# Performer on one Trainium2 core: ScalarE's square of a projection moved ahead of VectorE's rotation products, with a new order of all steps

## The chip, the cores and the metric

The kernel runs on one core of one Trainium2 chip. The metric is the time of one execution in device microseconds (us). Shorter is better. The engines are TensorE (PE, with its weight load PEld), VectorE (DVE), ScalarE (ACT), GpSimd (POOL) and SyncE (SP), which issues most transfers.

## What is computed

The program is a network of four layers on an input of 8 x 128 x 16 x 16, all in float32: an adder convolution, a Mamba layer of three scan branches, a layer of softmax attention with a mixture of experts, and a performer of eight layers with a spectral filter after it. The change lies in the attention of the performer. Per layer `i`, cut to what matters:

```python
q = (t @ Wq[i] + bq[i]);  k = (t @ Wk[i] + bk[i]);  v = (t @ Wv[i] + bv[i])
rot = stack((-t2[..., 1], t2[..., 0]))          # pairs of features exchanged
q = q * cos + rot(q) * sin                       # rotary, the same for k
dd   = (data * dn) @ proj.T                      # data: q or k, per head
diag = sum(data * data, -1) * 0.5 * dn * dn
out  = ratio * (exp(dd - diag - max(dd)) + eps)  # random features
ctx  = kp.T @ v;  o = (qp @ ctx) / (qp @ sum(kp))
t = t + o @ Wo[i] + bo[i];  t = t + gelu(layer_norm(t) @ W1) @ W2 + b2
```

A rotation does not alter the sum of squares of a pair, so the kernel takes `diag` from the square of the projection before it is rotated. That is why the square and the two rotation products read the same projection.

## The kernel before

The 2048 tokens are four blocks of 512 (two images each). A block is a Python generator, `_block`, which yields after each small step. It runs the third layer (`_layer2`), then eight performer layers (`_attention`, then the feed-forward part), then the end of the performer. Block 0 also prepares the weights of the next layer (`_weights_of`).

The order of the work is written out by hand: `AHEAD` runs thirty steps each of blocks 0 and 1 beside the Mamba layer, and then `ORDER`, a string of 1092 digits, says which block makes its next step. In it PE, DVE, ACT and POOL keep the order in which the steps were recorded (`manual_schedule`). So each engine works through one fixed queue, and an instruction that waits holds those behind it. A step of one block is never ahead of an earlier step of the same block; what the digits choose is how the four blocks interleave.

In `_attention`, `rotated(name)` is called for the key and, in the next step, for the query. It multiplies the normed state `u` by the weights into a bank of PSUM (`pa`), makes the two products with sine and cosine on VectorE (`ro`, L1565, and `rk` or `rq`, L1566), squares the projection on ScalarE (`sqk`, `sqq`; recorded at L1181 by the helper `act`), exchanges the pairs of `ro` (L1571) and adds (L1573). The step after the query's is the one that reads both squares:

```python
    pl = bank(S, [P, P], "pl3")
    for n, sq in enumerate((sqk, sqq)):
        for c in range(4):
            S.mm(pl[...], S.c("sel")[...], sq[:, c * P : (c + 1) * P], ...)
```

Each block has its own pools. `many` has three buffers for the tag "t", and `lsq3` (the squares of the state), `ro3`, `sqk`, `sqq`, and later `rd` take turns in them. `bank` takes one of the block's two PSUM banks. A helper `tables` loads another table on ScalarE when an activation needs a function that the present one lacks (exponential and logarithm in one, Gelu and tanh in the other); the page gives these loads the line L1173. All matmuls are recorded at L289.

Of the kernel before, what the change touches and what calls it, by code (L numbers as in the profile page):

```python
# [10 lines left out]
F32 = mybir.dt.float32  # L11
AF = mybir.ActivationFunctionType
# [4 lines left out]
P = 128  # L17
# [3 lines left out]
BLK = 512  # L21
# [270 lines left out]
def bc(ap, axis, n):  # L292

    a = ap.unsqueeze(axis)
    shape = list(a.shape)
    shape[axis] = n
    return a.to_broadcast(shape)
# [641 lines left out]
class _Fuse:  # L939
# [23 lines left out]
    def bank(self, shape, name):  # L963
        return self.psum.tile(shape, F32, tag="f", name=name)
# [133 lines left out]
def performer_layer(E, W):  # L1098
# [49 lines left out]

AHEAD = [t for i in range(30) for t in range(2) if i < (30, 30)[t]]
ORDER = [int(t) for t in (  # L1150
    "3203203322300231310203001302130303103023103020031203123012211001102001200310213200113301011301330203"
    "3203320312231233032123231223123233332332312312331231313232133213323032232202312320312021312221022110"
    "1322110231230212001020112032131303113023310032000201323001303202301201022120212033201320332203321300"
    "3200221022031022310233120020130012321031032100323003130130310320031033103201130323303021101120113301"
    "1332101220212002130212132301203222032200300220120112203210031203231010320011210130201130302101310230"
    "2101311301231013211022313223123132132133220133213003132103130221322013022013120231211312003121230032"
    "1103201230233110211331020001013002113001201032022320323021303323203220332130302002210220310223102312"
    "3002013001232103103210032300313030131030230103310320113012112002330133202212132320332113103131203031"
    "0231022023220122302230023210020313201320123312030323102132300300323313003311033112302012201330123122"
    "1031013121201220113210102002230220130221302113200203100321301230213031203102300201323100103320233320"  # L1160
    "20331031320132212032321023112222322132132213211201231123121021021132121312121013220130100213"
)]


# [4 lines left out]
def tables(S, name):  # L1169

    if S.table["now"] != name:
        S.table["now"] = name
        S.tc.keep_in_program_order(S.nc.scalar.preload_act_table_set(name))  # L1173


def act(S, out, src, func, **kw):
    if func in (AF.Exp, AF.Ln):
        tables(S, LN_EXP)
    elif func in (AF.Gelu, AF.Tanh):
        tables(S, GELU)  # L1180
    S.nc.scalar.activation(out, src, func, **kw)  # L1181
# [268 lines left out]
def _squares(S, h):  # L1450
    sq = S.many.tile([P, BLK], F32, tag="t", name="lsq3")
    act(S, sq, h, AF.Square)
    return sq
# [93 lines left out]
def _attention(S, i, H, sq, u, sums):  # L1547
# [6 lines left out]
    nc, one, two, many = S.nc, S.one, S.two, S.many  # L1554
# [4 lines left out]
    def rotated(name):  # L1559
        pa = bank(S, [P, 2, L], "pa3")  # L1560
        S.mm(pa.rearrange("p b l -> p (b l)"), w[name], u)
        bias = S.v(f"b{name}{i}")
        r = one.tile([P, 2, L], F32, tag="r" + name, name="r" + name)
        o = many.tile([P, 2, L], F32, tag="t", name="ro3")
        nc.vector.scalar_tensor_tensor(o, pa, bias, bc(S.c("sin"), 1, 2), ALU.add, ALU.mult)  # L1565
        nc.vector.scalar_tensor_tensor(r, pa, bias, bc(S.c("cos"), 1, 2), ALU.add, ALU.mult)  # L1566

        sq = many.tile([P, BLK], F32, tag="t", name="sq" + name)
        act(S, sq, pa.rearrange("p b l -> p (b l)"), AF.Square, bias=bias)
        o = o.rearrange("p b l -> p (b l)")  # L1570
        nc.vector.stream_shuffle(o, o, EXCHANGE)  # L1571
        r = r.rearrange("p b l -> p (b l)")
        nc.vector.tensor_add(r, r, o)  # L1573
        return r, sq

    k, sqk = rotated("k")
    yield
    q, sqq = rotated("q")

    ub = one.tile([P, 2, PAIR], F32, tag="ub", name="ub3")  # L1580
# [154 lines left out]
    sq = _squares(S, H)  # L1735
# [184 lines left out]
```

## Time and profile before

| what | value |
|---|---|
| median of 3 runs | 3007.63 us (3004.27 to 3009.06) |
| profiled execution | 3000.94 us, its span 2999.2 us |
| granted TensorE clock | 0.989 |
| busy in the span | PE 2854.1, DVE 2419.8, ACT 2273.2, POOL 699.6 us |
| loads of a ScalarE table | 134 in the profile, mean 1283 ns |
| a rotation product (L1565, L1566) | 744 and 742 ns, 64 of each |
| exchange and sum (L1571, L1573) | 723 and 692 ns, 64 of each |
| a square (`sqk`, `sqq`) | 684 and 682 ns, 32 of each |

The durations come from the one profiled execution. The span runs from the first to the last instruction of the profile. Time stands in order of the stages: the adder layer to about 1000 us, Mamba to about 1700, then the third layer and the performer to about 2760, then the spectral layer. In the tables of waits, "A <- B" says that A's engine stood idle and that B ended that. A busy PE is modelled: its matmuls are pipelined.

### The profile page before, as it was taken

How to read it: one execution, taken by the hardware profiler on the slowest of the kernel's cores; microseconds unless marked ns; L12 is line 12 of the kernel's file. 1: busy time of each engine (PE TensorE's matmuls, PEld its weight loads, DVE VectorE, ACT ScalarE, POOL GpSimd, SP SyncE). 2: the span in 40 equal slices, each digit the busy share in tenths (PEclk: the TensorE clock that was granted, in tenths of full speed). 3: DMA queues.
4: the chain of work that ended last, by engine and by line, in shares of the span. 5: the costliest groups of instructions: out<-in, count | busy, mean ns of one | idle time of the engine just before them, and what ended most of it. 6: DMA issues, size and time to landing. Idle time of an engine off the chain costs nothing.

```text
span 2999.2 us, 41845 instructions
## 1 busy us (share of the span) xinstructions
PE 2854.1 (95%) x16404; PEld 1275.4 (43%) x16404; DVE 2419.8 (81%) x3398; ACT 2273.2 (76%) x2744; POOL 699.6 (23%) x415
## 2 busy tenths in 40 slices
PE   9999999999999788998898998999999999999999
PEld 4222222222223333443343454455655555654444
DVE  8999999999997999999899658887777787784110
ACT  8999999999997777778777435578778778777332
POOL 0000000000000889998999400000000000000100
PEclk9999999999999999999999999999999999999999
DMA  2000000000000444344344200000000000001100
GB/s 68 1 1 5 1 1 5 1 2 5 1 1 16 169 149 148 135 149 141 133 157 137 84 29 1 14 1 14 14 14 1 14 14 1 14 1 53 43 29 14
DMA packets 39482, 133.46 MB, mean 44 GB/s; under 512 B 7522, under 2 KB 10732, under 8 KB 37748
## 3 DMA queue, kind: packets, MB, share of 16 engines
q1 hardware_dynamic: 38164, 129.46, 12.5%
q8 instruction: 129, 2.11, 0.3%
q10 hardware_dynamic: 1120, 1.32, 0.1%
q14 instruction: 69, 0.57, 0.1%
HBM read 127.88 MB, written 1.84 MB: 43 GB/s over the span
## 4 chain that ended last, share of the span: by engine, by line
PE 70%; DVE 16%; ACT 7%; POOL 3%; issue 3%; DMA 1%; DVEq 0%; ACTq 0%; POOLq 0%
PE o L289 30%; PE p L289 10%; DVE st L909 5%; PE acc L289 5%; PE g L289 4%; PE conv L289 3%; PE pc L289 2%; PE var L289 2%; PE pf L289 2%; POOL dbu L814 2%; PE pq L289 2%; PE pconv L289 1%; PE pn L289 1%; PE pa L289 1%; ACT da L827 1%
## 5 line engine op out<-in xcount | busy, mean ns | idle before, releaser
L289 PE MATMUL o<-d,sel 128*32 128x512 f32 x8512 | 921.5, 593 | 2.1 <-DVE d L446 1.2
L452 ACT ACTIVATE d<-sh,w 128x2048 f32<-128x2048 f32 x472 | 899.3, 1993 | 25.4 <-PE o L289 25.1
L450 DVE TENSOR_SCALAR d<-sh,w 128x2048 f32<-128x2048 f32 x592 | 718.4, 1281 | 11.0 <-PE o L289 10.9
L814 POOL TENSOR_TENSOR dbu<-du,bs 128x1024 f32<-128x1024 f32 x191 | 446.4, 2363 | 975.6 <-DVE du L786 970.1
L289 PEld LDWEIGHTS o<-d,sel 128*32 128x32 f32 x8512 | 278.6, 110 | 644.2 <-issue 523.0
L909 DVE TENSOR_TENSOR_SCAN st<-da,dbu 128x512 f32<-128x512 f32 x384 | 446.2, 1206 | 17.9 <-POOL dbu L814 13.8
L289 PE MATMUL acc<-st,cst 128*128 128x512 f32 x768 | 375.4, 621 | 52.8 <-DVE st L920 52.6
L827 ACT ACTIVATE da<-delta,neg_a 128x510 f32<-128x510 f32 x384 | 256.8, 684 | 79.1 <-DVE st L909 73.8
L289 PEld LDWEIGHTS acc<-st,cst 128*128 128x128 f32 x768 | 144.6, 196 | 252.7 <-issue 144.0
L920 DVE TENSOR_TENSOR st<-st,pcs 128x1024 f32<-128x1024 f32 x168 | 205.2, 1221 | 18.9 <-ACT pcs L819 1.6
L446 DVE SCALAR_TENSOR_TENSOR d<-sh,w,d 128x2048 f32<-128x2048 f32 x88 | 206.8, 2350 | 1.9
L1855 ACT COPY ug<-p 128x512 f32<-128x512 f32 x128 | 74.9, 585 | 136.7 <-PE p L289 136.7
L1173 ACT ACT_TABLE_LOAD x134 | 171.9, 1283 | 2.4
L1396 POOL TENSOR_TENSOR lw<-lw,turn 128x640 f32<-128x640 f32 x8 | 10.0, 1255 | 685.6 <-DVE turn L1395 592.6
L819 ACT COPY pcs<-cs 128x512 f32<-128x512 f32 x168 | 97.7, 582 | 54.2 <-DVE st L920 48.4
L289 PE MATMUL conv<-pad,f 128*128 128x512 f32 x288 | 135.0, 596 | 0.9 <-ACT pad L1071 0.5
L289 PE MATMUL p<-un,lw 128*128 128x512 f32 x256 | 123.7, 605 | 3.8 <-DVE un L1467 2.1
L289 PE MATMUL p<-g,lw 128*128 128x512 f32 x256 | 116.4, 597 | 3.9 <-ACT g L1181 3.9
L289 PE MATMUL p<-T,H 128*128 128x512 f32 x256 | 113.0, 600 | 0.8 <-DVE H L1784 0.8
L289 PE MATMUL g<-ug,me 128*128 128x512 f32 (+1 forms) x320 | 112.0, 509 | 0.0
L1181 ACT ACTIVATE ex<-ex 128x352 f32<-128x352 f32 x128 | 62.4, 494 | 51.6 <-DVE ex L1664 50.4
L289 PE MATMUL pf<-lw,rk 128*128 128x352 f32 x256 | 97.2, 476 | 0.5 <-DVE ek L1614 0.3
(366 smaller groups left out, 3898.6 us busy)
## 6 DMA issues: line engine op xcount, KB each, us to landing
bs<-rows SPq DMA_DIRECT2D x96, 512.0 KB, 3.8
cs<-rows SPq DMA_DIRECT2D x96, 512.0 KB, 4.6
m<-in_Mphi SPq DMA_DIRECT2D x8, 1024.0 KB, 4.9
lw<-in_layers SPq DMA_DIRECT2D x8, 948.0 KB, 4.7
f<-in_fuse SPq DMA_DIRECT2D x2, 1152.0 KB, 9.9
T<-in_T SPq DMA_DIRECT2D x1, 2064.0 KB, 7.4
diag<-in_diag SPq DMA_DIRECT2D x1, 1920.0 KB, 7.5
total<-sums SPq DMA_DIRECT2D x16, 64.0 KB, 2.0
```

The source lines that it names most:

```text
L289: self.nc.tensor.matmul(out, lhsT=lhsT, rhs=rhs, start=start, stop=stop)
L446: nc.vector.scalar_tensor_tensor(d, tap(k), wk, d, ALU.max, ALU.add)
L450: nc.vector.tensor_scalar(d, tap(k), wk, None, ALU.max)
L452: nc.scalar.activation(d, tap(k), AF.Abs, scale=-1.0, bias=wk)
L814: nc.gpsimd.tensor_tensor(dbs[r], got[r // NST]["du"], bc(row("bs", r), 1, 2), ALU.mult)
L819: nc.scalar.copy(pcs[r], row("cs", r))
L827: nc.scalar.activation(das[g % 3][:, :, 1:], d[:, :, 1:], AF.Exp, scale=a)
L909: nc.vector.tensor_tensor_scan(st[:, h, :], da, dbs[r][:, h, :], 0.0, ALU.mult, ALU.add)
L920: nc.vector.tensor_tensor(st, st, bc(pcs[r][:, :], 1, 2), ALU.mult)
L1173: S.tc.keep_in_program_order(S.nc.scalar.preload_act_table_set(name))
L1181: S.nc.scalar.activation(out, src, func, **kw)
L1855: nc.scalar.copy(dst, p4)
```

## The change

In `rotated`, the allocation of the square's buffer and the square itself now stand ahead of the two products and of their buffers. The string `ORDER` is a new one, of the same length and with the same number of each digit. Nothing else differs; the products are L1568 and L1569 in the changed file.

```diff
 ORDER = [int(t) for t in (
-    "3203203322300231310203001302130303103023103020031203123012211001102001200310213200113301011301330203"
+    "3203320320230231310231310032103210113132113200323020110302100123032102110031000113001320113322011303"
...
 )]
...
         pa = bank(S, [P, 2, L], "pa3")
         S.mm(pa.rearrange("p b l -> p (b l)"), w[name], u)
         bias = S.v(f"b{name}{i}")
+
+        sq = many.tile([P, BLK], F32, tag="t", name="sq" + name)
+        act(S, sq, pa.rearrange("p b l -> p (b l)"), AF.Square, bias=bias)
         r = one.tile([P, 2, L], F32, tag="r" + name, name="r" + name)
         o = many.tile([P, 2, L], F32, tag="t", name="ro3")
         nc.vector.scalar_tensor_tensor(o, pa, bias, bc(S.c("sin"), 1, 2), ALU.add, ALU.mult)
         nc.vector.scalar_tensor_tensor(r, pa, bias, bc(S.c("cos"), 1, 2), ALU.add, ALU.mult)
-
-        sq = many.tile([P, BLK], F32, tag="t", name="sq" + name)
-        act(S, sq, pa.rearrange("p b l -> p (b l)"), AF.Square, bias=bias)
         o = o.rearrange("p b l -> p (b l)")
         nc.vector.stream_shuffle(o, o, EXCHANGE)
```

More of the change, by code (lines that the diff above doesn't have):

```diff
@@ L1150 @@
 ORDER = [int(t) for t in (
-    "3203203322300231310203001302130303103023103020031203123012211001102001200310213200113301011301330203"
[L1152 to L1161, printed above, removed]
+    "3203320320230231310231310032103210113132113200323020110302100123032102110031000113001320113322011303"
+    "1133123001322302132321322332123323133230330213230123323233220230223322332230320320020133222032103210"
+    "2320011203002302021010212033023230300332003102103030113301210123013113320331103312301322132200231232"
+    "0302210032020030220302213032203123021332313031000200230311002103102110131201201230120133131131133121"
+    "3013210312232020320312300030231002032012032122020312001322012312023003320033211003210113021130323332"
+    "3320130221330232203232210323201132201320010011021210101310312010203010322010213003312231301331323101"
+    "2321012132001133101201033202101302110320112101201133203322113103132120201321201302200120200102201022"
+    "3101220132102311213011030020201010330230130233013320320310233121133113320313103321301322132200231232"
+    "0310220023020030202302231032203120231332310330100200320311002103120110311201123021132033210112112231"
+    "2133220321310312010202301120301020203100220120103122001103121123121310321230323123003113023312331131"
+    "13321321103032311020332212320213213020132212232203221022022032312203212112321032030232031322"
 )]
```

## The prediction

> **What bounds the kernel now.** I read the engine table first, then the busy time by stage, then waits and the chain of waits inside the stage the diff touches.
>
> ```profile
> span 2999.2 us, 41845 instructions
> PE 2854.1 (95%) x16404; PEld 1275.4 (43%) x16404; DVE 2419.8 (81%) x3398; ACT 2273.2 (76%) x2744; POOL 699.6 (23%) x415
> PE   9999999999999788998898998999999999999999
> ```
>
> TensorE works 95% of the span. The edit and the digit string act on the performer, roughly 1750 to 2750 us; layers 0 and 1 and the spectral layer keep their instructions.
>
> ```profile
> 1750.00:2000.00 250.00, 231.68 (x1047) 122.23 (x1046) 182.04 (x551) 124.16 (x222) 8.30 (x21) 0.99 0.04 13
> 2000.00:2250.00 250.00, 241.80 (x1459) 144.87 (x1459) 194.12 (x484) 193.51 (x309) 5.92 (x12) 0.99 0.04 13
> 2250.00:2500.00 250.00, 243.33 (x1465) 142.86 (x1464) 188.20 (x470) 197.80 (x313) 8.88 (x18) 0.99 0.02 9
> 2500.00:2750.00 250.00, 243.80 (x1402) 140.51 (x1401) 175.87 (x433) 196.88 (x308) 2.96 (x6) 1.00 0.02 8
> ```
>
> The columns are window, length, then busy time of PE, PEld, DVE, ACT, POOL. Over these 1000 us PE is busy 960.6, DVE 740.2 and ACT 712.4, so DVE idles 260 and ACT 288. PE sets the time, and only its waits can be won. A busy PE hides short gaps, so I also took the start of every matmul row from the timeline and subtracted the usual spacing of its form (429 ns for 128x512 pieces): between 1750 and 2760 us, 97 gaps exceed 0.3 us and hold **63.6 us**. Most shorter ones recur with the form (256 in `pn`, 49 us) and no order removes them.
>
> Now who waits at the squares (answer of the waits view: engine, tile, line <- releaser: total us, times, longest):
>
> ```profile
> ACT sqk L1181 <- DVE rk L1566: 26.1, 22, 5.5
> ACT sqq L1181 <- DVE rq L1566: 14.8, 16, 1.5
> PEld pl L289 <- ACT sqq L1181: 8.9, 9, 2.0
> PE pl L289 <- ACT sqq L1181: 6.6, 6, 1.7
> ```
>
> ScalarE stands 40.9 us in 38 cases because VectorE has not finished its second product from the same projection `pa`, and then TensorE waits for ScalarE. The chain of waits shows both ways on:
>
> ```profile
> 2010.30 0.66 DVE ro L1565
> 2010.96 0.67 DVE rq L1566
> 2011.66 0.05 issue
> 2011.71 0.70 ACT sqq L1181
> 2012.41 0.04 issue
> 2012.45 0.42 PE pl L289 x8
> ...
> 2219.27 0.69 ACT sqk L1181
> 2219.96 0.02 issue
> 2219.97 1.28 ACT L1173
> ```
>
> Two products (start, length in us), the square, then PE; or, below, the square and then ACT's own queue, here a table load. In ten windows of 100 us the chain passes 31 of the 64 squares; in 24 the piece before is L1566, and 3 of those 24 go straight on to `pl`, 21 stay on ACT.
>
> **What the Trainium skill says.** (1) "PSUM — Partial Sum Buffer", section on bank collisions: two engines on one bank and quadrant at once is an error, reads against reads included. So the program must order square and products; moving the square reverses a wait, it does not delete one. The trace agrees as far as it goes: those 40.9 us of waits; no run shows the error. (2) "Perfetto Trace Analysis", section on the DVE / Act instruction: a wait FIFO stands before the engine. I take it that a waiting instruction holds what is queued behind it, as above, where the table load follows the late square. (3) "ScalarE: Activation LUTs", "What ACT_TABLE_LOAD costs": 1283 ns, plus a drain of about 1380 ns. The trace agrees on the first (134 loads, mean 1283 ns); the drain is not seen: ACT idles 2.4 us in all before them.
>
> **The change part by part.** The sum stands against the profiled execution, 3000.94 us (span 2999.2 and 1.7 around it), which ran 6.7 us under the median 3007.63; I carry the difference to the median.
>
> *Square ahead, waits on PE.* No instruction is added or removed; 64 squares lose two products (L1565 744 ns, L1566 742 ns; 1.33 us on the chain, where they overlap). By start spacing, PE's gaps over 0.3 us at the `sqq` half of `pl` are 7, together 8.5 us. The longest, 1.95 us, is little more than 1.43 (products and hand-over), so some remains. I take 6 of 8.5: **-6.0** (bounds 0 and -8.5).
>
> *Square ahead, ACT's queue.* ACT idles 27.1 us before `sqk` and 19.6 before `sqq`, 46.7 together. What that is worth on PE is not shown by any row. At most the chain's 24 passages, 24 x 1.43 = 34 us; at least nothing, if the next wait ends as late. For a middle I use the stage's own exchange rate: 63.6 us of PE gaps stand against 260 + 288 = 548 us of DVE and ACT idle time, 0.116 us per us. 46.7 x 0.116 = **-5.4** (0 to -25, the 34 without the PE gaps).
>
> *VectorE's new waits.* L1568 (L1565 before) now waits for the square: 684 ns and about 0.1 hand-over. Before, the 64 first products waited only 1.7 us for `pa`, in 3 cases: VectorE comes late to them anyway, so only a square that ACT reaches late costs. From 0 to 64 x 0.79 = 51 us of DVE time; I take a quarter, 13. A second wait is not in the diff. The three buffers of tag "t" are shared by `lsq3`, `sqk`, `ro3`, `sqq`: with each square allocated before its `ro3`, the query's `ro3` often gets the buffer of `sqk`. Resolving the built program's semaphores to the instruction that raises them, **18 of 32** query rotations wait for `pl`'s matmuls that read `sqk`, an instruction of the block's next step; before, none did. In these 18 the key's rotation lies directly ahead on DVE (744+742+723+692 ns = 2.9 us), with 0.8 for its square; the query projection ends 0.86 us (two 429 ns pieces) after the key's, so DVE arrives about 2.8 us after it. PE work between that projection and `pl` is 1.1 to 5.4 us in the new order; counting 0.4 for `pl` itself and hand-over, the excess over 2.8 sums to 0.4x2 + 1.0x5 + 1.25x2 + 2.3x2 + 3.0 = 16 us (six lie below). Behind L1568 stand the rest of the rotation, `ub`, and other blocks' `mq`, `ks`, `H`, `dg`, for which PE waits. 13 + 16 = 29 us at 0.116: **+3.4** (0 to +29).
>
> *Table loads.* The new digits need 132 loads in the program against 136: 4 x 1.283 = 5.1 us of ACT. ACT L1173 is 2.8% of the chain in the stage, 28 us of its 172, so 0.16 x 5.1 = **-0.8** (0 to -5.1).
>
> *The new order.* The multiset of digits is the same (276, 252, 282, 282), as are all matmuls, products and DMAs; each block's steps stay in sequence. PE work between the query's projection and `pl` falls from a median of 4.5 to 3.65 us, for the key's from 8.6 to 4.8. Before, that chain needs 0.74 + 0.74 + 0.69 + 0.2 = 2.4 us and 4 of 32 have less; now it needs 0.9 and none has less. SP's eight layer loads keep their order, and POOL its preparation; they have lw's second buffer and layers of about 100 us as cover (4.7 us to land). On SP, two Mphi loads pass ahead of Mu, in a stage where PE's gaps total under 2 us from 2800 on. All other pairings of blocks are dealt anew, and no row of before prices that: bounds -15 and +15 of the 63.6 us of gaps; I take 0.
>
> Sum: -6.0 - 5.4 + 3.4 - 0.8 = **-8.8**; 3000.94 - 8.8 = 2992.1, and by the median 3007.63 - 8.8 = 2998.8, rounded 2999.
>
> **The rivals.**
> *Nothing to measure* (0.22): a square released early meets the next late input, and PE, 96% busy, gives back only its direct gap, while the new waits cost that. For it: 55 of the 63.6 us of gaps lie elsewhere. Against: 24 passages of the chain. -2: 3006.
> *Slower: VectorE held at L1568* (0.28). The mechanism is the buffer wait on `pl`, with the square's wait, on an in-order queue 74% busy. Gains are 12.2 us; it decides when more than 12.2 / 29 = 42% of the added DVE time reaches PE. At 70% it costs 20: +8, **3016**. For it: the new waits close a loop PE-DVE-PE that did not exist. Against: DVE has 260 us of idle time, and the pairs now stand together.
> *More comes back* (0.12): half the chain's 34 us, with the order helping: -20, 2988. For it: the passages come in all layers. Against: PE's own waits at `pl` are only 8.5 us.
> That the change does not do what it says, a square first in the text but reached late by ACT, would show as long waits of L1568 for ACT and belongs to the slower case.
>
> **How the numbers follow.** The forecast has 0.38. 0.2% of the time is 6 us, about what a measurement of this kernel tells from none. Faster 0.38 + 0.12 = 0.50, same 0.22, slower 0.28. The likeliest case alone spans 2990 to 3004 (its unknowns, ACT's queue and the order); over all cases 2983 to 3018: it takes in the slower rival's centre and the larger gain's, leaving 0.1 on each side.
>
> **What would show it.** Right: the waits of `sqk` and `sqq` for L1566 (40.9 us) are gone, `pl` waits for `sqq` under 3 us, table loads show 4 fewer, L1568 waits for `sqk`, `sqq` and `pl` under 35 us, PE idles some 9 us less between 1750 and 2760, and all earlier stages agree. Wrong: the time moves outside the performer; or L1568's waits exceed 50 us and PE's waits on DVE tiles (`un`, `rd`, `y`) grow; or the idle time before the squares is gone and PE's gaps are not smaller.

## The result, and the profile after

The changed kernel took 2993.02 us (median of 6 runs, 2988.05 to 2994.82) against 3005.95 us for the kernel before in the same comparison: 12.9 us faster, a ratio of 0.9953 with a 95% interval of 0.9943 to 0.9963. A second, later comparison gave 0.9948 (0.9935 to 0.996). Forecast were 8.8 us.

The head of the page after, to be laid beside the one before:

```profile
span 2993.0 us, 41823 instructions
PE 2857.9 (95%) x16404; PEld 1281.7 (43%) x16404; DVE 2421.7 (81%) x3398; ACT 2268.3 (76%) x2740; POOL 700.4 (23%) x415
PE   9999999999999788998898998999999999999999
```

The same matmuls and the same VectorE operations; ScalarE has four instructions fewer. Where the time went shows by stage. From the last `conv` matmul to the first one of the spectral layer the kernel before took 973.6 us and the changed one 962.6 (958.5 when it was run again), 11.0 us less. The two spans differ by only 6.2 us, because the changed kernel's profile entered that stage 5.5 us later. I take that for chance: 4.2 of the 5.5 us stood already at the end of the adder layer, which is alike in all kernels and ended anywhere from 946.9 to 953.8 us in the profiles shown here. So I compare medians, and in the profiles this stage alone. The matmuls of the spectral layer took 233.7 and 233.0 us.

The windows of the stage (window, length, busy PE, PEld, DVE, ACT, POOL):

```profile
1750.00:2000.00 250.00, 233.87 (x1008) 126.22 (x1007) 175.58 (x536) 119.59 (x222) 8.32 (x21) 0.97 0.04 13
2000.00:2250.00 250.00, 244.06 (x1511) 147.96 (x1510) 197.98 (x495) 189.37 (x311) 5.94 (x12) 1.00 0.04 13
2250.00:2500.00 250.00, 243.20 (x1464) 142.13 (x1463) 189.78 (x473) 202.22 (x317) 8.90 (x18) 1.00 0.03 9
2500.00:2750.00 250.00, 246.65 (x1421) 143.94 (x1420) 180.26 (x445) 199.35 (x313) 3.59 (x7) 1.00 0.02 5
```

PE is busy 967.8 of 1000 us, 7.2 more than before. These windows are fixed and the stage is not, so the stage itself is the better measure: from `conv` to the spectral layer PE stood idle 42.9 us before and 33.0 after. PE's gaps over 0.3 us, taken from the starts of its matmuls as in the prediction but over this stage, fell from 64.6 us (98 gaps) to 51.5 (85). Both falls, 9.9 and 13.1 us, answer to the stage's 11.0.

The waits at the squares, in the views of the waits after (engine, tile, line <- releaser: total us, times, longest):

```profile
DVE ro L1568 <- ACT sqk L1181: 31.0, 27, 2.8
DVE ro L1568 <- ACT sqq L1181: 10.2, 8, 1.6
ACT sqk L1181 <- PE pa L289: 3.2, 6, 1.3
ACT sqq L1181 <- PE pa L289: 0.4, 2, 0.2
PE pl L289 <- DVE rk L1569: 2.9, 6, 0.6
```

ScalarE's 40.9 us of waits for the second product are gone; before its squares it now waits for the projection alone, 3.6 us. In their place **VectorE stands 41.2 us** (31.0 and 10.2) before its first product. The last line shows where this reaches TensorE: `pl` takes the PSUM bank that the key's projection had, and the last to read that bank is now the key's second product and no longer the square. The chain of waits shows the turn (start, length in us):

```profile
2150.44 0.59 ACT sqk L1181
2151.03 0.03 issue
2151.05 0.75 DVE ro L1568
2151.80 0.60 DVE rk L1569
2152.40 0.72 DVE ro L1571
```

The square comes first and the products follow it. In the same ten windows as before the chain passes 30 squares, where it passed 31, and 17 of the 30 lead straight to `ro`. So the wait was turned round, at almost the same length. Then why is the kernel faster? These traces alone don't say; the experiments go further.

### The profile page after: what moved, and what is told of

It reads as the page before. It is cut to its first block, busy times and chain, and to the rows that moved or that the text cites. A ratio compares the mean times of both kernels' runs of the same rounds, so it can differ in the third digit from the quotient of the medians.

```text
span 2993.0 us, 41823 instructions
## 1 busy us (share of the span) xinstructions
PE 2857.9 (95%) x16404; PEld 1281.7 (43%) x16404; DVE 2421.7 (81%) x3398; ACT 2268.3 (76%) x2740; POOL 700.4 (23%) x415
## 4 chain that ended last, share of the span: by engine, by line
PE 68%; DVE 15%; ACT 9%; POOL 4%; issue 3%; DMA 1%; DVEq 0%; ACTq 0%; POOLq 0%
PE o L289 29%; PE p L289 8%; DVE st L909 5%; PE acc L289 5%; PE g L289 4%; PE conv L289 3%; PE pc L289 2%; PE var L289 2%; PE pf L289 2%; POOL dbu L814 2%; PE pa L289 1%; ACT L1173 1%; PE pq L289 1%; ACT da L827 1%; PE pconv L289 1%
## 5 line engine op out<-in xcount | busy, mean ns | idle before, releaser
L1173 ACT ACT_TABLE_LOAD x130 | 166.8, 1283 | 2.3
```

## The experiments

Each was measured beside the kernel before, and the ratios are to it. The stage times and PE gaps are those from the last `conv` to the spectral layer.

### Each half of the change alone

**The square ahead, in the old order:**

```diff
 # the changed kernel, with
-ORDER = <the new string>
+ORDER = <the string of before>
```

> The square ahead of the products, with the order of steps of before. Theory A (the freed wait of ScalarE carries the gain): most of the 12.9 us comes back by the square alone, 6 to 10 us, ratio 0.9967 to 0.998; ScalarE's 41 us of waits for L1566 gone, PE gaps over 0.3 us down from 64.6 to about 56. Rival B (the gain is the new order's): within 3 us of before, ratio 0.999 to 1.001. Rival C (the old order does not suit the new waits): slower by 3 us or more, because VectorE stands at L1568 for squares that ScalarE reaches late.

Measured: 3063.3 us, ratio 1.0201 (1.0187 to 1.0214), 58 us slower than before. VectorE's waits in that kernel:

```profile
DVE ro L1568 <- ACT sqk L1181: 43.6, 30, 3.4
DVE mq L1661 <- PE pq L289: 39.5, 37, 6.6
DVE rd L1730 <- ACT rd L1181: 33.0, 15, 5.7
DVE ro L1568 <- ACT sqq L1181: 27.0, 22, 3.4
```

VectorE now stands 70.6 us before its first products. PE's gaps rise from 64.6 to some 119 us, most of it not where `pl` reads the squares (1.0 us left there) but elsewhere: `var` 20.2 us, `pg` 13.9, `pn` 10.7, `pq` 9.9. I take most of these for what VectorE delivers late or lets ScalarE have late; `pn` is another matter, as shown below. Theories A and B both fail; C holds, and far beyond its 3 us.

**The new order, with the square behind:**

```diff
 # the kernel before, with
-ORDER = <the string of before>
+ORDER = <the new string>
```

> The new order of steps, with the square behind the products as before. Theory A: the order was made around the early square, and without it ScalarE waits again some 40 us or more, so 0 to 5 us slower than before, ratio 1.000 to 1.002. Rival B (the new order's own merit, such as four table loads fewer): 8 to 13 us faster, ratio 0.9957 to 0.9973.

Measured: 3076.44 us, ratio 1.0245 (1.023 to 1.0261), 71 us slower. PE's waits:

```profile
PE pl L289 <- ACT sqq L1181: 39.4, 23, 2.3
PE p L289 <- ACT g L1181: 16.2, 15, 1.8
```

PE's gaps are 136.9 us, 45.5 of them before the query half of `pl`, and ScalarE waits 93.2 us for L1566 (44.5 and 48.7). Its profile has the four table loads fewer of the new order (130 for 134), so these alone don't carry the gain. Theory A had the direction, but at most 5 us of it.

Each half alone loses 2% or more; both together win half a per cent. They are not two gains that add up.

**The clock in these kernels.** Not all of the two losses is waiting. The traces also record the clock that TensorE was granted, and in them it is either full or half. A window of the kernel with the order alone; the third number from the end is the granted clock:

```profile
2250.00:2500.00 250.00, 230.06 (x1242) 128.76 (x1240) 168.93 (x417) 180.19 (x278) 5.94 (x12) 0.93 0.03 9
```

It was 0.99 in this window before. Summed over the stage, the half clock lasted 10.2 us before and 17.1 in the changed kernel (6.8 when it was run again), but 58.0 with the square alone and 78.5 with the order alone. While it lasts, the 128x512 matmuls start 853 ns apart instead of 429. I estimate that half of the added time, some 24 and 34 us, is matmuls made slower; PE's busy time in the stage, for the same matmuls, rose with it from 930.7 us to 957.1 and 961.0. PE's gaps count such slow matmuls too: 25 of the 119 us and 45 of the 137 fall in half clock, `pn` in the first kernel almost wholly. The half clock comes in the kernels where PE waits most. Whether the waits bring it on, no run here shows; so the 58 and 71 us are prices of these kernels and not of their waits alone.

### One square of the two

```diff
+        def square(): ...          # allocation and activation as before
+        if name == "q":
+            sq = square()          # "k" in the other kernel
         nc.vector.scalar_tensor_tensor(o, pa, ...)
         nc.vector.scalar_tensor_tensor(r, pa, ...)
+        if name != "q":
+            sq = square()
```

> New order, only the query's square ahead, the key's behind its products as before. The order alone cost PE 45 us of gaps in front of the query half of pl, so theory A (the query's square is what the new order leans on): most of the change is kept, within 10 us of the changed kernel, ratio 0.994 to 0.999; VectorE's 31 us before the key's first product go, ScalarE's wait for the key's second product comes back (some 40 us). Rival B (both squares matter, because a late key square delays the query's on ScalarE's queue): 20 us or more slower than the changed kernel, ratio over 1.002.

New order, query only: 3008.73 us, ratio 1.0011 (1.0004 to 1.0019). That lies between the two theories: from the order alone the query's square brings 68 us, and the key's square on top of it some 17 more (3008.73 against 2991.78 in the same comparison). PE's gaps before the `sqq` half of `pl` are 4.1 us.

> Old order, only the query's square ahead. With both ahead the old order lost 58 us, VectorE idle 44 us before the key's first products and 27 us before the query's. Theory A (each reversed wait costs in proportion to VectorE's idle time): 27 of 71 us of it, so about 20 us slower than before less what pl gains (8 us): ratio 1.002 to 1.007. Rival B (the key's wait alone did the harm): within 3 us of before or faster, 0.996 to 1.001.

Old order, query only: 3048.49 us, ratio 1.0145 (1.013 to 1.0161). Slower than either theory said. VectorE waits 55.7 us for `sqq` in 29 cases, where with both squares ahead it waited 27.0; the share of a wait in one kernel does not give its cost in another. The half clock lasts 47.8 us here.

> New order, only the key's square ahead, the query's behind its products as before. The order alone (both behind) stood at 1.0245 with 45 us of PE gaps before the query half of pl, the query's square alone ahead at 1.0011. Theory A (the query's late square is what breaks the new order): those gaps are back, at least 40 us, and the time is near the order alone, 1.015 to 1.025. Rival B (the two squares add up): the key gives what was left, 0.5%, so about 1.019 or below, with the gaps before sqq clearly fewer than 40 us, and in the limit 1.005.

New order, key only: 3096.81 us, ratio 1.0306 (1.0293 to 1.0319), worse than no square ahead at all, which neither theory had. ScalarE's waits:

```profile
ACT sqq L1181 <- DVE rq L1574: 96.8, 32, 4.4
ACT ex L1181 <- DVE ex L1671: 54.5, 62, 4.0
```

All 32 query squares wait, 3.0 us each. VectorE waits 30.8 us for the key's squares before its first products; I take it that the query's products come later for that, and the query's square behind them. PE's gaps before the `sqq` half are 60.8 us, and the half clock lasts 112.6 us. Theory A's place is right (the query's late square), its size too small.

### No wait between the two at all

To price the wait in each order I let the square read another tile, the normed state `u` in SBUF. ScalarE has the same number of squares (707 ns each), but neither engine waits for the other over the projection. The bank of the projection is then also freed by the products alone, so what this takes away is the sharing as a whole.

```diff
-        act(S, sq, pa.rearrange("p b l -> p (b l)"), AF.Square, bias=bias)
+        act(S, sq, u, AF.Square, bias=bias)
```

> The kernel before, but the squares are taken of the normed state u in place of the projection (the diagonal term is then another one): same work on ScalarE, but it waits for nothing that VectorE does, and VectorE waits for nothing of it. Old order. Theory A: the wait of ScalarE costs before 6 to 12 us of time; ratio 0.996 to 0.998, and PE's waits at pl for sqq are gone. Rival B: the next wait ends as late; within 3 us, ratio 0.999 to 1.001.

Old order: 2984.9 us, ratio **0.9941** (0.9927 to 0.9954). The stage takes 955.1 us, PE's gaps are 46.3, those at `pl` 3.9. Theory A has the direction, but the size lies above its range, and PE's waits at `pl` are halved and not gone.

> The changed kernel with its new order, but the squares are taken of the normed state u in place of the projection (the diagonal term is then another one): neither engine waits for the other over the projection. The changed kernel shows VectorE idle 41 us before its first products, in place of ScalarE's 41 us before. If that reversed wait still costs time (theory): 5 to 10 us faster than the changed kernel, ratio to before 0.992 to 0.994. Rival (it falls into VectorE's slack and costs nothing): as the changed kernel, 0.9945 to 0.9963.

New order: 2972.24 us, ratio **0.989** (0.9876 to 0.9903). The stage takes 946.1 us, PE's gaps are 39.8. The four windows summed:

```profile
sum 1000.00, PE 975.85 PEld 562.22 DVE 757.07 ACT 723.20 POOL 33.43; mean PE 243.96 PEld 140.56 DVE 189.27 ACT 180.80 POOL 8.36
```

PE is busy 975.9 of 1000 us, but the stage ends at 2735 us here, so the last 15 us of these windows belong to the spectral layer. In the stage itself PE stands idle 24.2 us, against 28.9 in the old order with the square of `u`. The theory holds, and again the wait costs more than the range of it: 0.9948 against 0.989 is 17 us.

These two show where most of the gain lies. Three ways to measure it, in us:

| what is compared | ratios, of 3005 us | medians | stage in the profiles |
|---|---|---|---|
| wait taken away, old order | 17.7 | 20.2 | 18.5 |
| wait taken away, new order with the square ahead (against the changed kernel run again) | 17 | 19.5 | 12.4 |
| old order to new, no such wait in either | 15 | 12.7 | 8.9 |
| the change itself, first and second comparison | 14, 16 | 12.9, 13.3 | 11.0, 15.1 |

**The wait costs much the same in both kernels, whoever waits**: 18 to 20 us in the old order, 12 to 20 in the new. What differs is the rest of the order. Without any such wait the new one stands at 0.989 / 0.9941 = 0.9949 of the old, where the change itself stands at 0.9948 and 0.9953. So by ratios and medians turning the wait round gained next to nothing in itself, and by the stage of one profile each some 6 us. Each ratio is known to about 4 us and a difference of two to about 6, so these readings don't contradict one another: the better order holds the larger part of the gain, and whether the turned wait is a few us cheaper stays open.

The new order can bear the wait on VectorE and not on ScalarE, as the kernel with the order alone shows. The prices are not exact for another reason. The square of `u` can start a little earlier than one of the projection could, which makes them too high; and new waits come in, which makes them too low (VectorE then stands 4.7 us before its first products for `pl` in the new order, and ScalarE 4.5 us before `sqq` for VectorE's `rk` in the old).

### The buffer wait

```diff
-        sq = many.tile([P, BLK], F32, tag="t", name="sq" + name)
+        if name == "k":
+            sq = one.tile([P, 4, HM], F32, tag="ek", name="sqk").rearrange("p c m -> p (c m)")[:, 0:BLK]
+        else:
+            sq = many.tile([P, BLK], F32, tag="t", name="sqq")
```

> The changed kernel, with the key's square in the room of ek (unused until the step after the squares are read) in place of a buffer of tag t: no query rotation waits any more for the matmuls that read sqk (18 of 32 did). Theory: that wait is hidden (the trace of the changed kernel shows it once, 0.6 us), so within 3 us of the changed kernel, ratio to before 0.9943 to 0.9963. Rival (the buffer wait costs the 3.4 us or more of the prediction, unseen because it is put down to the square): 3 to 8 us faster than the changed kernel, ratio 0.9927 to 0.9943.

2986.84 us, ratio 0.9945 (0.9932 to 0.9958). None of the 32 query rotations waits for `pl` in the built program now, where 18 did, and VectorE's waits for the squares stay (30.9 and 10.2 us). The changed kernel run again stood at 0.9948:

> The changed kernel once more, beside the other kernels of this call on the same chip: 0.9943 to 0.9963 of before, as in the first comparison; a base for differences of a few us.

2991.78 us, 0.9948 (0.9935 to 0.996). The two intervals lie over each other, so the buffer wait costs nothing that these runs can tell; a cost of up to some 4 us isn't excluded. In the changed kernel's trace it shows once, with 0.6 us. Part of the reason is that VectorE stands at the square instead: with the square of `u` in the new order, where that wait is gone, the buffer wait shows 7 times, 4.7 us together.

### GpSimd squares the rotated key

A rotation keeps the sum of squares of a pair, so the key's square can be taken after it, from SBUF, by an engine that is nearly idle here:

```diff
+        if name == "k":                       # at the end of rotated
+            sq = many.tile([P, BLK], F32, tag="t", name="sq" + name)
+            nc.gpsimd.tensor_tensor(sq, r, r, ALU.mult)
```

> The kernel before, old order, but GpSimd squares the rotated key (the same sum over a pair) from SBUF; the query's square stays on ScalarE behind its products. So no engine waits over the key's projection, and ScalarE loses 32 squares (22 us). Theory (what costs is one engine waiting for the other over the bank): ScalarE's 26 us of waits go, the key has 8.6 us of PE work until pl at the median against some 4.5 that the longer way needs; of the 18 to 20 us that the square of u brought in this order about half to all, ratio 0.994 to 0.997. Rival (pl now waits for GpSimd): PE gaps at pl for sqk of 10 us and more, ratio over 1.000.

Old order: 2997.7 us, ratio 0.9976 (0.9964 to 0.9988). Faster than before by some 7 us, less than expected: ScalarE's 26.1 us of waits for the key's products went with its key squares, but before `sqq` its wait for L1566 rose from 14.8 us to 31.7:

```profile
  DVE rq L1566: 31.7, 22
```

No longer held at the key, ScalarE comes to the query's square earlier and is held there. PE's gaps at that half of `pl` stay at 8.6 us; GpSimd needs 1041 ns a square, and PE's gaps at its half are 2.8 us. So a part of the wait was handed on within ScalarE's queue, and neither the theory nor the rival had that.

> The changed kernel, new order, query's square ahead on ScalarE, and GpSimd squares the rotated key from SBUF. VectorE's 31 us of waits for the key's square go, but the new order leaves 4.8 us of PE work between the key's projection and pl at the median, as long as the way over GpSimd (0.75 + 0.74 + 0.72 + 0.69 + some 1.2), and under 4 us in 13 of 32 cases. Theory: pl now waits for the key in many of them, PE gaps at pl of 15 us or more, and the time is 5 to 25 us above the changed kernel, ratio 0.996 to 1.004. Rival (freeing VectorE is worth more): faster than the changed kernel, under 0.993.

New order: 3005.33 us, ratio 0.9997 (0.9988 to 1.0005). PE's gaps before the key half of `pl` are 29.8 us in 19 cases; this is the theory's loss, in its range. VectorE no longer waits for the key's square (9.7 us for the query's remain), but that square comes too late for `pl`.

### Work put into VectorE's wait

```diff
+    ub = ...                    # two VectorE operations that need only sums
     k, sqk = rotated("k")
     yield
     q, sqq = rotated("q")
-    ub = ...
```

> The changed kernel, with the two small VectorE operations that make ub (260 ns each, they need only the sums of the normed state) recorded ahead of the key's rotation in place of behind the query's, so that they fill VectorE's wait for the key's square (31 us in 27 cases, 1.15 us each). Theory: the reversed wait costs about 17 us for its 41 us (the squares of u in the new order), 0.42 us per us; up to 14 us of work moved into it give 3 to 6 us against the changed kernel, ratio to before 0.9925 to 0.994. Rival 1 (the wait is simply shorter, VectorE was not what limits there): as the changed kernel, 0.9943 to 0.9958. Rival 2 (the order leans on ub's old place, as on all else): over 0.998.

2987.43 us, ratio 0.9934 (0.9917 to 0.9952). VectorE's wait before the key's products fell from 31.0 to 21.4 us and the stage from 958.5 to 956.0 (changed kernel run again). It is the fastest kernel here whose computation is whole, by its ratio, but its interval covers the changed kernel's 0.9948. Whether it beats that one is open; the rival "over 0.998" is out.

## Why the prediction was right, and where it was not

The direction and the size held: -8.8 forecast, -12.9 measured, inside 2983 to 3018. The forecast's signs in the profile came true in part. The waits for L1566 went, there are four table loads fewer, PE idles 9.9 us less in the stage where some 9 were forecast, and the earlier stages agree but for the 5.5 us named above. PE's matmuls of `pl` no longer wait for `sqq` at all, though their weight loads do, 4.2 us where under 3 were asked for; what holds the matmuls is the key's second product, 2.9 us. VectorE's waits at L1568 were to stay under 35 us and were 41.8. The working behind the sum was wrong in three terms that made up for each other, so that the sum came out near is in good part luck: it laid the gain to the square released early, and the runs lay most of it to the order, which stood at nothing.

- **Waits on PE at `pl`, -6.0.** PE's gaps at the two halves of `pl` fell from 8.5 us to 4.2, now at the key half. About 4 us, less than the 6 taken but within its bounds.
- **ScalarE's queue, -5.4.** Removing that wait in the old order, with nothing put in its place, gave 18 to 20 us, of which 4.6 lie at `pl`. The term was too small by more than a factor of two. The exchange rate of 0.116 us of PE time per us of engine idle time was the fault; measured are 0.4 to 0.5 (18 to 20 us for 40.9). The average spreads PE's gaps evenly over all idle time. I take it that an engine's idle time just before an instruction that the chain passes counts for more than the rest; no run tests that.
- **VectorE's new waits, +3.4.** I took 29 us of waiting, 13 for the square and 16 for the buffer, and 0.116 us each. Measured were 41.2 and 0.6. The buffer's 16 us were argued from distances in PE's order; the kernel with the key's square elsewhere shows no cost that can be told, for VectorE comes to the buffer later than I assumed, held by the square. The square's wait cost 12 to 20 us for 41, about 0.4 us per us. With the two terms before, the turned wait nets to somewhere between zero and -6, where I had -8.0.
- **The new order, 0.** This is the term furthest off. I allowed ±15 us and put nothing in the sum, as if the order could be added to the square. The order alone costs 71 us, the square alone 58, both together gain 13. There is no value for either by itself. Compared in kernels where neither engine waits for the other, the new order is worth 9 to 15 us, which is most of the gain or all of it.
- **Table loads, -0.8.** The profile shows 130 loads where there were 134, mean 1283 ns as before. No run isolates them; the order alone had them and lost.

The slower rival named the right engine and the right line: VectorE held at L1568. In the old order it did just that, at 2.0% and not the 0.3% I gave it. In the new order it holds VectorE too, at a price of 12 to 20 us, and the gain stands beside it. Its mechanism was only half right: the square's wait did the holding, not the buffer wait on `pl`. "Nothing to measure", at 3006 us, lies outside the measured interval.

What stays open: which pairings of the new order are worth its 9 to 15 us. From the kernel before to the changed one the fall of PE's gaps is spread over `p`, `px`, `pl` and `po`, a few us each, with rises at `pm`, `pf` and `pw`. No run here takes them apart. Open too is how much of the large losses is the clock.

## What to carry to other kernels

A written-out order of instructions fits one set of waits. Judge a change of a wait and the order together, and be ready for one to lose without the other, as here (58 and 71 us) even where both together gain 13. Moving a shared read ahead of another engine's reads turns a wait round, so price the turned wait with the same rate as the one that goes; the cheapest way here to learn that rate was a run in which neither waits. Before a loss is put down to waits, look at the granted clock as well.

What would gain from such a pair is less clear. Taking the sharing away gained 12 to 20 us, but in kernels that compute something else. Of the kernels with the computation whole, the one with GpSimd for the key gained some 7 us in the old order and lost some 14 in the new, and work put into the wait gained nothing that can be told from the changed kernel.

## What the runs showed of the hardware that I had not expected

The same ScalarE square took 671 to 688 ns (medians) when it read the projection from PSUM and 707 ns when it read `u` from SBUF. A GpSimd product of a 128x512 tile with itself, in SBUF, took 1041 ns, 1.5 times VectorE's 692 ns for a sum of the same shape; other GpSimd operations on two tiles of this shape took 1267 to 1270 ns in an earlier stage of the kernel before. The half clock of TensorE came in stretches of 3.4 to 10.2 us inside a stage where PE worked most of the time: 2 to 5 of them in the kernels within 1.2% of the kernel before, 11 to 22 in the four slower ones.
